# Whole-row accumulations, a fifth product buffer and later gate sums in a Mamba, attention and expert kernel on one core

## The chip, the core and the metric

The kernel runs on one core of one Trainium2 chip, as one launch. The metric is the device time in microseconds; lower is better. The time before is 3446.69 us, the median of three runs (3444.32 to 3450.47). The core has the engines PE (TensorE matmul, with PEld for its weight loads), DVE (VectorE), ACT (ScalarE), POOL (GpSimd) and SP (SyncE, which here only issues DMAs).

## The reference, cut to what matters

The input is 8 images of 256 channels by 32 x 32, that is 8 sequences of 1024 tokens. Layer 0 is a Mamba block and an MLP; layer 1 is attention and a mixture of experts. All is float32. The part that the change touches is the scan of the Mamba block:

```python
xz = x @ W_in
xm, z = jnp.split(xz, 2, axis=-1)            # d_inner = 512 each
xm = silu(causal_conv4(xm) + conv_b)
dt, Bm, Cm = jnp.split(xm @ W_x, [16, 32], axis=-1)
dt = softplus(dt @ W_dt + b_dt)
A = -jnp.exp(A_log)                           # (512, 16)
def step(h, inputs):
    dt_t, B_t, C_t, x_t = inputs
    dA = jnp.exp(dt_t[..., None] * A)
    h = dA * h + (dt_t * x_t)[..., None] * B_t[:, None, :]
    y = jnp.einsum('bds,bs->bd', h, C_t)
    return (h, y)
_, ys = jax.lax.scan(step, h0, seq)
y = (ys + xm * D_param) * silu(z)
x = y @ W_out + residual
# then: x = gelu(layernorm(x) @ W1 + b1) @ W2 + b2 + x
# layer 1: t = t + attention(ln(t)); t = t + experts(ln(t)), two of eight experts per sequence
```

## The kernel before, in words

A sequence is cut into two chunks of 512 tokens, so there are 16 chunks, `i = 0..15`; an even one is a first chunk (`c = 0`) and an odd one the second chunk of its sequence. Channels lie on the 128 partitions, 512 inner channels being four groups, handled as two halves `h` of two groups. A tile of a half is 128 partitions by 2 x 512 values, 0.5 MB.

The scan is written as a stream of 512 steps. A chunk has 32: 16 states `s`, and for each both halves. Step `g` consists of these VectorE operations, written out by hand in the main loop at the end of the function:

- `inputs(g + 1)`: the B product, `hb <- xm,bc`, into a buffer `hb` of the pool `h4`
- `scan(g, q)`: the recurrence by `tensor_tensor_scan`, in place in `hb`, with the decays `da_all` that ScalarE makes in `decay`. A first chunk starts at state zero, and both groups of a half go through one scan of 1024 columns (the first decay of the second group is zero). A second chunk needs two scans of 512, each from the `state` that the first chunk left. In a first chunk GpSimd copies the last column to `state`.
- `sums(g)`: the C product in place in `hb`, and then a DMA issued by GpSimd that adds `hb` to `dx`, the accumulator `me["acc", h]` of this chunk and half. When it has landed the buffer goes back to `h4`.

Sixteen states are thus summed by 512 accumulating DMAs of half a megabyte. `h4` has four buffers. In a first chunk the C product and the DMA leave out the last column (511 of 512), because `state` takes it before the product; the epilogue adds it separately: `yl` is `state` times the last row of C, summed over the states into the accumulator's last column.

Everything else is put around the stream. Each other piece of work is a Python generator: `prologue(i)` (projection, convolution, time step `dt`; ends with `xm <- xm,dt`), `gate_part(i)` (the gate), `epilogue(i)` (output projection and MLP), `attention`, `experts`, `setup` (weights and edge bias, including `column_bias`), and `park`. `park` runs through chunks 2 to 15 once, early and at lowest urgency: it makes their x projection and gate, and stores them in DRAM (`xin_d`, `sz_d`), from which the prologue and `gate_part` load them. The time step needs logarithms, and adds their parts by DMAs issued by GpSimd (`dt <- e`, `dt <- u`).

The order in which generators are advanced is set at build time by a small planner: `Model` and `Queue` keep a clock per engine from fixed prices, `advance()` takes all generators that are due, in order of urgency, until the clock of the work has reached VectorE's (`vec.at`); `keep_warm()` puts filler matmuls (`warm`) where TensorE would stand idle. Each engine then runs its instructions in the order emitted. Four tables of one number per chunk steer it: `FRONT[i]` is the step of chunk `i` in which `prologue(i + 1)` starts, `GATE[i]` that in which `gate_part(i)` starts, `CONV[i]` puts the convolution on TensorE instead of VectorE, and `SOFT[i]` makes a prologue use one more accumulating DMA per half in place of one VectorE operation. `Slots` hands out buffers: `now()` takes the one that is free first, even if that lies ahead of the planner's clock.

At the start the first chunk's input and the weights are loaded. `fold(w, n, gain, ...)` multiplies columns of the input weights `w_in` by the layer norm's gain and makes their column sums with the shift on TensorE (`b_in <- vecs,w_in`, matmuls of one column): once for the x half and, first in `setup`, once for the gate half. `setup` is advanced once while the loads are issued, which emits the gate's column sums.

Of the kernel before, what the change touches and what calls it, by code (L numbers as in the profile page):

```python
# [9 lines left out]
F32 = mybir.dt.float32  # L10
# [3 lines left out]
ALU = mybir.AluOpType  # L14
AX = mybir.AxisListType
PSUM = bass.MemoryType.PSUM

P = 128
B, C, L = 8, 256, 1024
KC = C // P  # L20
CH = 512
NCH = L // CH
DI, NS, RK, KW = 512, 16, 16, 4
ND = DI // P
# [3 lines left out]
NHALF = ND // 2  # L28
# [26 lines left out]
def hybrid_kernel(ctx: ExitStack, tc: tile.TileContext, a: dict, out: bass.AP):  # L55
# [80 lines left out]
    def load(name, shape, src):  # L136
        t = const.tile(shape, F32, name=name, tag=name)
        loads.append((t, src))
        return t
# [7 lines left out]

    work = ctx.enter_context(ExitStack())
    work.enter_context(tc.manual_schedule(engines=set(ENGINES)))
    w_in = load("w_in", [P, KC, 2 * DI], a["W_in"].rearrange("(k p) n -> p k n", p=P))  # L150

    w_x = const.tile([P, ND, 4 * RK], F32, name="w_x")
    w_dt = const.tile([3 * RK, NHALF, P], F32, name="w_dt")
# [114 lines left out]
    T4, H4, PT, AHEAD, LAG, TICK = 25, 4, 4, 2, 8.0, 0.15  # L268


    FRONT = (5, 5, 4, 4, 1, 13, 15, 1, 13, 1, 11, 1, 4, 5, 9)
    GATE = (27, 5, 30, 30, 30, 17, 28, 11, 28, 27, 9, 22, 29, 28, 10, 26)
    CONV = (0, 0, 0, 0, 1, 0, 0, 0, 0, 0, 0, 1, 0, 1, 0, 0)
    SOFT = (1, 1, 1, 1, 0, 0, 0, 0, 0, 0, 0, 0, 0, 0, 0, 0)

# [251 lines left out]
    def fold(w, n, gain, shift, bias, name, first=0):  # L529


        ps = sbank(f"{name}_{first}")
        cols = slice(first * P, (first + n) * P)
        for o in range(n):
            for k in range(KC):
                pe.matmul(
                    ps[:, o : o + 1], w[:, k, cols][:, o * P : (o + 1) * P], V(shift, k),
                    start=(k == 0), stop=(k == KC - 1),
                )
        yield  # L540
        if name == "b1":
            vec.tensor_tensor(bias, ps[:, :n], V("b1"), ALU.add)
        else:
            vec.tensor_copy(bias[:, first : first + n], ps[:, :n])
        for k in range(KC):
            vec.tensor_scalar(w[:, k, cols], w[:, k, cols], V(gain, k), None, ALU.mult)
# [137 lines left out]
    def prologue(i: int):  # L684
# [23 lines left out]
        def skip_path():  # L708

            for h in range(NHALF):  # L710
                dx = me["acc", h] = yield from mem.take(f"dx_{i}_{h}")
                for r in range(2):
                    act.activation(
                        dx[:, r, :], xm[h][:, r, :], AF.Identity, scale=V("D", 2 * h + r)
                    )

        if i == 0:
            yield from skip_path()
# [160 lines left out]
    def place(g):  # L879
        i, k = divmod(g, NSTEP)  # L880
        s, h = divmod(k, NHALF)
        return i, s, h
# [18 lines left out]
    def inputs(g):  # L901

        i, s, h = place(g)
        hb = hbs[g] = h4.now(f"hb_{g}")
        bc, landed = bcs[g // NHALF]
        vec.at = max(vec.at, landed)
        xd = chunk[i]["xd"][h]
        vec.tensor_tensor(hb, xd, bc[:, 0, :].unsqueeze(1).to_broadcast([P, 2, CH]), ALU.mult)
        if s == NS - 1:
            t4.put(xd)  # L910
# [24 lines left out]
    def sums(g):  # L935

        i, s, h = place(g)
        me = chunk[i]
        bc, _ = bcs[g // NHALF] if h < NHALF - 1 else bcs.pop(g // NHALF)
        hb = hbs.pop(g)  # L940
        n = CH if i % NCH == NCH - 1 else CH - 1
        y = hb[:, :, :n]
        vec.tensor_tensor(y, y, bc[:, 1, :n].unsqueeze(1).to_broadcast([P, 2, n]), ALU.mult)
        model.t = vec.at
        me["landed", h] = pool.dma_start(out=me["acc", h][:, :, :n], in_=y, accum_op=ALU.add)
        h4.put(hb, at=me["landed", h])

    parked, parked_x = {}, set()
# [1 line left out]
    def park():  # L950

        for i in range(PARK, B * NCH):
            b, c = divmod(i, NCH)
            sz_d = dram.tile([NHALF, P, 2, CH], F32, name=f"sz_d_{i}", tag=f"sz_d_{i}")
            mem = Owner(t4, 3)
            xn = yield from mem.take(f"xe_{i}")
            yield sp.dma_start(xn, x_v[b, :, :, c * CH : (c + 1) * CH])
            xn = yield from layernorm(mem, banks, xn, xn, f"a{i}", kept=i)
            yield
            xi = yield from gates(i, mem, xn, 0)  # L960
            yield
            for h in range(NHALF):
                mem.put(
                    xi[h], at=sp.dma_start(xin_d[b][h, :, :, c * CH : (c + 1) * CH], xi[h])
                )
            parked_x.add(i)
            sz = yield from gates(i, mem, xn)
            mem.put(xn)
            for t in sz:
                act.activation(t, t, AF.Silu)  # L970
            lnexp()
            yield
            for h in range(NHALF):
                mem.put(sz[h], at=sp.dma_start(sz_d[h], sz[h]))
            mem.end()
            parked[i] = sz_d

    def gate_part(i):

# [22 lines left out]
    def gates(i, mem, xn, first=ND):  # L1002

        while first and not gates_ready:
            yield POLL
        sz, ps = [], None
        for d in range(ND + 1):
            if d:
                h, q = divmod(d - 1, 2)
                act.activation(  # L1010
                    sz[h][:, q, :], ps, AF.Identity, bias=b_in[:, first + d - 1 : first + d]
                )
                banks.put(ps)
            if d < ND:
                if d % 2 == 0:
                    sz.append((yield from mem.take(f"z{first}_{i}_{d // 2}")))
                ps = yield from banks.take(f"z{first}_{i}_{d}")
                for k in range(KC):
                    pe.matmul(
                        ps, w_in[:, k, (first + d) * P : (first + d + 1) * P], xn[:, k, :],  # L1020
                        start=(k == 0), stop=(k == KC - 1),
                    )
                yield
        return sz

    def epilogue(i: int):
# [9 lines left out]
        y = me["sz"]  # L1036
        if c < NCH - 1:
            for h in range(NHALF):
                yl = work_pool.tile([P, NS + 1, 2], F32, name=f"yl_{i}_{h}", tag="yl")
                vec.tensor_tensor(  # L1040
                    yl[:, 1:], state[:, :, 2 * h : 2 * h + 2],
                    me["c_last"].unsqueeze(2).to_broadcast([P, NS, 2]), ALU.mult,
                )
                vec.tensor_reduce(
                    yl[:, 0], yl[:, 1:].rearrange("p s d -> p d s"), AX.X, ALU.add
                )
                y_end = me["acc", h][:, :, CH - 1]
                vec.tensor_tensor(y_end, y_end, yl[:, 0], ALU.add)
        for h in range(NHALF):
            yield me["landed", h]  # L1050
            vec.tensor_tensor(y[h], me["acc", h], y[h], ALU.mult)
            t4.put(me["acc", h])
        yield
# [1006 lines left out]
    with tc.tile_pool(name="work", bufs=1) as work_pool:  # L2060
# [86 lines left out]
        def setup():  # L2147
            mem = Owner(t4, 9)
            tiles = []
            for n in range(9):  # L2150
                tiles.append((yield from mem.take(f"setup_{n}")))
            held = []
            for n in range(2):
                held.append((yield from pairs.take(f"setup_p{n}")))
            pl = Scratch([t4.of[id(t)][1] for t in tiles])
            yield from fold(w_in, ND, "ln1_g", "ln1_b", b_in, "b_in", ND)
            gates_ready.append(True)
            yield
            yield from column_bias(pl)
            yield  # L2160
            eye = pl.tmp("eye", [P, P], F32)
            make_identity(nc, eye)
            blk = pl.tmp("eye_b", [P, HD], F32)
            yield
            for r in range(4):
                rows = slice(HD * r, HD * r + HD)
                vec.tensor_copy(blk[rows, :], eye[rows, rows])
            vec.tensor_tensor(
                taps, blk.unsqueeze(1).to_broadcast([P, ND * KW, HD]),
                V("conv_w").unsqueeze(2).to_broadcast([P, ND * KW, HD]), ALU.mult,  # L2170
            )
            vec.tensor_tensor(pick3, eye[:, 0:4], eye[:, 4:8], ALU.add)
            vec.tensor_tensor(pick3, pick3, eye[:, 8:12], ALU.add)
            set_up.append(True)
            yield
            yield from fold(w1, HID // P, "ln2_g", "ln2_b", b1, "b1")
            yield
            yield from bounds(pl)
            yield
            yield from values_bias(pl)  # L2180
            expert_constants(pl)
            mem.put(*tiles)
            mem.end()
            pairs.put(*held)
# [9 lines left out]
        next(first)  # L2194
        for n, (t, src) in enumerate(loads):
            sp.dma_start(t, src)
            if n == 2:
                next(second)

        folding = fold(w_in, ND, "ln1_g", "ln1_b", b_in, "b_in")  # L2200
        for n in range(8):
# [329 lines left out]
```

## Time and profile before

| What | Value |
|---|---|
| median of three runs | 3446.69 us |
| the profiled execution itself | 3453.02 us |
| its span, first to last instruction | 3451.2 us |
| mean granted TensorE clock | 0.954 |
| PE busy | 3158.2 us, 92% |
| DVE busy | 2994.9 us, 87% |
| ACT busy | 2461.8 us, 71% |
| POOL busy | 1136.1 us, 33% |
| DMA | 667.94 MB, queue 0 (issued by POOL) 57.9% and queue 1 (by SP) 25.1% of 16 engines |

The page of a profile cuts the span into 40 slices and gives each engine's busy share of a slice in tenths. Its groups of instructions name engine, operation and tiles (output, arrow, inputs), with busy time and mean duration, and then the idle time of the engine just before them and what ended it. Nearly all instructions go through one recording helper, so all have its line and the tile names tell them apart. For a DMA the last number is the median time from issue to landing. Durations come from one execution, which took 6.3 us longer than the median. Idle time of an engine that doesn't set the pace costs nothing.

### The profile page before, as it was taken

Reading aid. Unit: us, or ns where it says so; the run is one execution under the profiler, and the core shown is the slowest. Engines: PE = TensorE matmul, PEld = TensorE weight load, DVE = VectorE, ACT = ScalarE, POOL = GpSimd, SP = SyncE. Lnnn points to the kernel's source line nnn. Section 1 sums busy time; section 2 is a strip of 40 time slices with the busy share of each in tenths; the row PEclk is TensorE's granted clock in tenths of the full one; section 3 lists DMA queues with packets and bytes.
Section 4 is the critical chain, followed back from the end, with each engine's and each line's share of the span. In section 5 each row is a group of like instructions: output and inputs, shape, how many; then the busy total and the mean of one; then the engine's idle time right before and its main releaser. Section 6 shows DMA issues by size and latency. Waiting matters only on the chain. (4 is left out here: it accounts for less than half of the span.)

```text
span 3451.2 us, 44547 instructions
## 1 busy us (share of the span) xinstructions
PE 3158.2 (92%) x16321; PEld 1383.4 (40%) x16321; DVE 2994.9 (87%) x3140; ACT 2461.8 (71%) x3594; POOL 1136.1 (33%) x1072
## 2 busy tenths in 40 slices
PE   7888878899999998999999899999899999999997
PEld 5544343433344433433443334333333343335343
DVE  5989999899999979999999999999899899962561
ACT  4667757678868887787768767877768877764643
POOL 0243135312452235332542244225422553311010
PEclk9878998999999999999989999999999999999999
DMA  3888898989899989888998999899978998863140
GB/s 117 224 198 192 201 235 208 223 214 224 200 247 220 239 188 213 198 200 200 220 238 195 210 238 223 191 201 233 205 184 198 232 216 199 209 150 97 32 99 24
DMA packets 248629, 667.94 MB, mean 194 GB/s; under 512 B 31184, under 2 KB 108112, under 8 KB 248400
## 3 DMA queue, kind: packets, MB, share of 16 engines
q0 software_dynamic: 138880, 373.62, 57.9%
q1 hardware_dynamic: 109520, 291.38, 25.1%
q8 instruction: 130, 2.13, 0.2%
q14 instruction: 99, 0.81, 0.1%
HBM read 269.20 MB, written 92.93 MB: 105 GB/s over the span
## 5 line engine op out<-in xcount | busy, mean ns | idle before, releaser
L95 POOL DMA_DIRECT2D dx<-hb x512 | 541.9, 1064 | 1559.2 <-DVE hb L98 1094.7
L98 ACT ACTIVATE da_all<-dt,vecs 128x512 f32<-128x512 f32 (+1 forms) x1024 | 697.2, 716 | 341.8 <-DVE hb L98 333.5
L98 DVE TENSOR_TENSOR hb<-xm,bc 128x1024 f32<-128x1024 f32 x512 | 616.5, 1204 | 52.2 <-DMA dx<-hb 34.2
L98 DVE TENSOR_TENSOR_SCAN hb<-da_all,state,hb 128x512 f32<-128x512 f32 x512 | 631.3, 1268 | 6.4 <-ACT da_all L98 6.4
L98 DVE TENSOR_TENSOR hb<-hb,bc 128x1024 f32<-128x1024 f32 (+1 forms) x512 | 622.4, 1216 | 0.0
L98 DVE TENSOR_TENSOR_SCAN hb<-da_all,hb 128x1024 f32<-128x1024 f32 x256 | 585.0, 2285 | 9.7 <-ACT da_all L98 9.5
L98 ACT ACTIVATE pt<-sc 128x1024 f32<-128x1024 f32 x512 | 494.0, 1017 | 72.0 <-PE sc L98 61.3
L98 PE MATMUL warm<-mean_c,zero_c 128*128 128x256 f32 x1168 | 375.2, 444 | 61.6 <-ACT dt L98 12.0
L98 POOL COPY state<-hb 128x2 f32<-128x2 f32 x256 | 353.7, 1383 | 205.5 <-DVE hb L98 192.2
L98 PE MATMUL sc<-qk,qk 32*128 32x512 f32 x2048 | 327.7, 645 | 11.8 <-ACT pt L98 10.7
L98 PEld LDWEIGHTS warm<-mean_c,zero_c 128*128 128x128 f32 x1168 | 221.1, 210 | 220.5 <-PE warm L98 81.0
L98 PE MATMUL num<-pt,v 128*32 128x512 f32 x2048 | 276.8, 610 | 7.4 <-DVE ot L98 5.9
L98 PE MATMUL facc<-fh,w 128*128 128x512 f32 x512 | 245.5, 630 | 17.4 <-ACT he L98 4.5
L98 PE MATMUL fh<-x_f,w 128*128 128x512 f32 x480 | 232.8, 615 | 10.5 <-DVE x_f L98 5.0
L98 PE MATMUL den<-pt,ecb 128*32 128x512 f32 x1792 | 236.8, 599 | 0.0
L98 PE MATMUL re<-he,g 128*128 128x512 f32 x472 | 216.4, 602 | 10.0 <-ACT x L98 4.2
L98 PE MATMUL he<-xe,g 128*128 128x512 f32 x448 | 219.4, 615 | 4.6 <-DMA xe<-xf_d 4.2
L98 PE MATMUL z<-sq_a,w_in 128*128 128x512 f32 x448 | 216.1, 615 | 3.0 <-ACT z L98 1.2
L98 ACT ACT_TABLE_LOAD x159 | 204.0, 1283 | 3.4 <-PEq L2518 0.7
L98 PEld LDWEIGHTS sc<-qk,qk 32*128 32x128 f32 x2048 | 97.0, 185 | 181.8 <-issue 74.6
L98 PEld LDWEIGHTS facc<-fh,w 128*128 128x128 f32 x512 | 100.0, 202 | 148.6 <-issue 121.3
L98 PEld LDWEIGHTS fh<-x_f,w 128*128 128x128 f32 x480 | 86.0, 191 | 146.6 <-issue 106.3
(410 smaller groups left out, 4141.1 us busy)
## 6 DMA issues: line engine op xcount, KB each, us to landing
bc<-bc_d SPq DMA_DIRECT2D x256, 512.0 KB
dx<-hb POOLq DMA_DIRECT2D x256, 512.0 KB, 7.1
dx<-hb POOLq DMA_DIRECT2D x256, 511.0 KB, 8.0
dt<-e POOLq DMA_DIRECT2D x36, 512.0 KB, 7.7
dt<-u POOLq DMA_DIRECT2D x30, 512.0 KB, 10.8
xin_d<-z SPq DMA_DIRECT2D x28, 512.0 KB
sz_d<-z SPq DMA_DIRECT2D x28, 512.0 KB
sz<-sz_d SPq DMA_DIRECT2D x28, 512.0 KB
```

The costliest lines, as they stand in the source:

```text
L95: f(*args, **kw)
L98: return f(*args, **kw)
```

## The change

- `sums` adds the whole `hb` to the whole accumulator in first chunks as well. The last column then receives values of no meaning. The prologue saves the last column of the freshly made `dx` in a small tile `dx_end` (one ACT copy per half), the epilogue reduces `yl` into the same tile, and after the accumulations have landed it overwrites the accumulator's last column with the sum of both.
- The input weights become two tiles, `w_in` (x half) and `w_z` (gate half), each with its load. When `park` and the first two gates are done, `w_z` is no longer read and joins `h4` as a fifth buffer. `inputs` moves the planner's VectorE clock on to the time when a buffer is free.
- The gate's column sums are no longer emitted while the loads are issued. They come when `setup` is first advanced.
- `FRONT`, `GATE`, `CONV` and `SOFT` have other values.

```diff
-    w_in = load("w_in", [P, KC, 2 * DI], a["W_in"].rearrange("(k p) n -> p k n", p=P))
+    w_in = load("w_in", [P, KC, DI], a["W_in"].rearrange("(k p) n -> p k n", p=P)[:, :, :DI])
+    w_z = load("w_z", [P, KC, DI], a["W_in"].rearrange("(k p) n -> p k n", p=P)[:, :, DI:])
...
-    FRONT = (5, 5, 4, 4, 1, 13, 15, 1, 13, 1, 11, 1, 4, 5, 9)
-    GATE = (27, 5, 30, 30, 30, 17, 28, 11, 28, 27, 9, 22, 29, 28, 10, 26)
-    CONV = (0, 0, 0, 0, 1, 0, 0, 0, 0, 0, 0, 1, 0, 1, 0, 0)
-    SOFT = (1, 1, 1, 1, 0, 0, 0, 0, 0, 0, 0, 0, 0, 0, 0, 0)
+    FRONT = (7, 13, 4, 4, 1, 14, 10, 1, 13, 1, 10, 6, 1, 5, 10)
+    GATE = (20, 4, 30, 30, 22, 7, 30, 18, 28, 25, 5, 28, 30, 30, 12, 26)
+    CONV = (0, 0, 0, 1, 1, 0, 0, 0, 0, 0, 0, 0, 0, 1, 0, 0)
+    SOFT = (1, 0, 0, 1, 0, 0, 0, 0, 1, 0, 1, 0, 0, 0, 0, 0)
...
+                if c < NCH - 1:
+                    if h == 0:
+                        me["dx_end"] = work_pool.tile(
+                            [P, 2, NHALF, 2], F32, name=f"dxe_{i}", tag="dxe", bufs=2
+                        )
+                    act.copy(me["dx_end"][:, 0, h, :], dx[:, :, CH - 1])
...
     def inputs(g):
         i, s, h = place(g)
+        vec.at = max(vec.at, min(h4.free)[0])
         hb = hbs[g] = h4.now(f"hb_{g}")
...
-        me["landed", h] = pool.dma_start(out=me["acc", h][:, :, :n], in_=y, accum_op=ALU.add)
+        me["landed", h] = pool.dma_start(out=me["acc", h], in_=hb, accum_op=ALU.add)
...
+        while not {("g", i) for i in range(PARK)} <= done:
+            yield POLL
+        make = h4.make
+        h4.make = lambda nm, k: w_z if k == H4 else make(nm, k)
+        h4.free.append((model.t, H4))
...
                 vec.tensor_reduce(
-                    yl[:, 0], yl[:, 1:].rearrange("p s d -> p d s"), AX.X, ALU.add
-                )
-                y_end = me["acc", h][:, :, CH - 1]
-                vec.tensor_tensor(y_end, y_end, yl[:, 0], ALU.add)
+                    me["dx_end"][:, 1, h], yl.rearrange("p s d -> p d s"), AX.X, ALU.add
+                )
         for h in range(NHALF):
             yield me["landed", h]
+            if c < NCH - 1:
+                vec.tensor_tensor(
+                    me["acc", h][:, :, CH - 1], me["dx_end"][:, 0, h], me["dx_end"][:, 1, h],
+                    ALU.add,
+                )
...
-            yield from fold(w_in, ND, "ln1_g", "ln1_b", b_in, "b_in", ND)
+            yield from fold(w_z, ND, "ln1_g", "ln1_b", b_in, "b_in", ND)
...
         for n, (t, src) in enumerate(loads):
             sp.dma_start(t, src)
-            if n == 2:
-                next(second)
```

More of the change, by code (lines that the diff above doesn't have):

```diff
@@ L532, in fold @@
         ps = sbank(f"{name}_{first}")
-        cols = slice(first * P, (first + n) * P)
+        cols = slice(0, n * P)
         for o in range(n):
@@ L1019, in gates @@
                     pe.matmul(
-                        ps, w_in[:, k, (first + d) * P : (first + d + 1) * P], xn[:, k, :],
+                        ps, (w_z if first else w_in)[:, k, d * P : (d + 1) * P], xn[:, k, :],
                         start=(k == 0), stop=(k == KC - 1),
@@ L1038, in epilogue @@
             for h in range(NHALF):
-                yl = work_pool.tile([P, NS + 1, 2], F32, name=f"yl_{i}_{h}", tag="yl")
+                yl = work_pool.tile([P, NS, 2], F32, name=f"yl_{i}_{h}", tag="yl")
                 vec.tensor_tensor(
-                    yl[:, 1:], state[:, :, 2 * h : 2 * h + 2],
+                    yl, state[:, :, 2 * h : 2 * h + 2],
                     me["c_last"].unsqueeze(2).to_broadcast([P, NS, 2]), ALU.mult,
```

## The prediction

> **What bounds the kernel now.** I read the busy slices first, then busy time by stretches of the span, then what VectorE waited for in each stretch. The times give where the scans begin (74.8 us) and where VectorE's last scan ends (about 3066). Columns of the first block: stretch and its length, busy time of PE, PEld, DVE, ACT, POOL with instruction counts, TensorE clock, DMA share, GB/s.
>
> ```profile
> 0.00:75.00 75.00, 54.67 (x273) 35.88 (x275) 38.72 (x70) 30.74 (x49) 1.71 (x16) 0.89 0.41 128
> 75.00:325.00 250.00, 211.57 (x1192) 122.72 (x1189) 219.24 (x280) 163.37 (x342) 90.51 (x94) 0.86 0.80 196
> 325.00:1263.00 938.00, 849.82 (x4195) 374.07 (x4194) 878.17 (x820) 704.32 (x1009) 300.51 (x279) 0.95 0.91 218
> 1263.00:3068.00 1805.00, 1685.03 (x8937) 687.73 (x8936) 1714.79 (x1687) 1372.91 (x1947) 703.12 (x643) 0.96 0.93 211
> 3068.00:3451.00 383.00, 357.09 (x1738) 163.04 (x1737) 143.97 (x286) 190.45 (x249) 40.22 (x41) 0.99 0.27 64
> ```
>
> Three stages follow. A start of 75 us; a stream of 512 scan steps, 75 to 3068, in which VectorE is busy 219 + 878 + 1715 = 2812 of 2993 us, so it sets the pace and leaves 181 us idle; and a tail of 383 us in which TensorE is busy 357. TensorE's share in the stream is 92%, part of it `warm` filler. So a gain must come out of the 181 us, or out of the start.
>
> VectorE's waits in the stream from 1250 on (waited for: total us, times, longest), then the group that waits, from the page:
>
> ```profile
> DVE hb L98 <- DMA dx<-hb: 26.3, 15, 4.8
> DVE xm L98 <- DMA dt<-u: 12.2, 2, 10.3
> DVE hb L98 <- issue: 10.2, 4, 4.0
> DVE sz L98 <- DMA dx<-hb: 4.2, 2, 2.7
> ...
> L98 DVE TENSOR_TENSOR hb<-xm,bc 128x1024 f32<-128x1024 f32 x512 | 616.5, 1204 | 52.2 <-DMA dx<-hb 34.2 <-issue 18.1
> dx<-hb POOLq DMA_DIRECT2D x256, 512.0 KB, 7.1
> dx<-hb POOLq DMA_DIRECT2D x256, 511.0 KB, 8.0
> ```
>
> The reader is to see one product, `hb<-xm,bc`, waiting 52 us in all for a free `hb` buffer: the accumulating DMA that last read it hasn't landed. Between a product's hand-over and the reuse of its buffer four steps later VectorE has three scans, two B products and two C products: 3 x 2.29 + 2 x 1.20 + 2 x 1.22 = 11.7 us. Issue (0.9 to 1.2 us) and landing (median 7 to 8, longest 17.3) mostly fit in that, so the waits are short and scattered.
>
> DMA by chunk; queue 0 in a first chunk (1630 to 1817), then in the second chunk after it (1817 to 1989), with packets, MB, share:
>
> ```profile
> q0 software_dynamic: 11298, 25.48, 74.4%
> ...
> q0 software_dynamic: 6259, 22.16, 65.3%
> ```
>
> With queue 1 (25.8%) the first chunk's engines are at 100%.
>
> The start and one chunk border (start us, us, engine, what, idle before it):
>
> ```profile
> 8.22 3.55 PE L98 MATMUL b_in<-vecs,w_in 128*128 128x1 f32 x16 [8.22 <-DMA w_in<-in_W_in]
> 11.70 1.08 PE L98 MATMUL mu_a<-xn,mean_c 128*32 128x128 f32 x16
> ...
> 1232.36 1.23 DVE L98 TENSOR_TENSOR xm<-xm,dt 128x1024 f32<-128x1024 f32 x1 [8.18 <-ACT dx L98]
> ```
>
> The first line are the gate's column sums; the mean of the first chunk stands behind them in TensorE's order. The last is part of the largest stall, 1212 to 1237: the time step of chunk 6 isn't ready.
>
> **What the Trainium skill says.** "DMA: Bandwidth & Descriptors", section "SWDGE vs HWDGE vs iDMA": an accumulating DMA can be issued from GpSimd only, and packets of up to 4096 B are preferred. The trace agrees on the first: all 512 stand in POOL's queue. A whole row pair is 4096 B, a cut one two pieces of 2044 B; the packet counts above fit that. The same page, "Anatomy of one DMA", gives 2.0 us + bytes/436e3, an estimate of 3.2 us for 512 KB. The trace has 7.1: engines that are 90% busy queue. The section "Why small descriptors are slow" says that SBUF-to-SBUF transfers don't suffer from small pieces; the trace differs (8.0 against 7.1 us, and the next part), and I take the trace.
>
> **The change part by part**, against the profiled execution (3453.0 us, span 3451.2; 6.3 above the median of 3446.7).
>
> *Whole rows.* 256 accumulations turn from 2 x 2044 B to 4096 B per partition. Price: queue 0 took 0.744 x 187 x 16 = 2226 engine-us in the first chunk, 0.653 x 172 x 16 = 1797 in the next. At the latter's 81 per MB the former's 25.48 MB would cost 2066: 160 less. Three later pairs give 145, 129 and 238. Of a chunk's 184 x 16 = 2944 that is 4 to 8 points of share. Issue on POOL falls from 1.20 to 0.86 us (its medians in a first and a second chunk). Neither is on VectorE's path; they make landings earlier by about 0.9 us. Before 1250 this alone acts on 15.7 us of `hb` waits (52.3 - 36.5): I take -5; bounds 0 and -10. Waits of `sz` and `dt` on DMAs (4.2 and 15.7 in the stream): -5, bounds 0 and -10; the 10.3 us one at 2698 comes behind a row of gathers on POOL, which stays.
>
> *Fifth slot.* By the recorded order of the changed program 63 of the 512 products use the second half of the input weights, the first in step 196 (about 1285 us). A fifth slot adds one step, 2.29 + 1.20 + 1.22 = 4.7 us, to the 11.7. The longest wait after 1250 is 4.8 us; only where two follow within two steps does something remain (I keep 3). So 36.5 - 3: -34. Lower bound of the gain: no DMA lands earlier, and waits pass on to the serial accumulation per `dx` half (POOL waited 275 us for it in 69 cases), half, -17; upper -36.
>
> *Gate sums later.* TensorE's mean no longer stands behind 3.55 us of sums and the wait to 8.2. The input's DMA issues at 1.2 us, ahead of the weights; at the 330 GB/s and more that this stretch moves, its 0.5 MB have landed by about 5.5 to 6. The next join is `var_a` at 18.4, behind the other column sums, which stay and need only half the weight bytes. I take -5, bounds -2 and -7. The moved sums land among filler after the first convolution, which covers them; the weight load becomes two DMAs on SP (one more issue, 0.5 us, with the small loads behind it; none is needed before 40 us). Two foldings of 0.48 us stay where they were on VectorE.
>
> *The last column.* 16 ACT copies of about 0.19 us: 3 us on an engine busy 76%, hidden; cover gone, +3. VectorE's three small operations per half (0.19 + 0.19 + 0.16) stay in number; the last now follows the landing, which the product after it waits for anyway: 0.
>
> *Planner and tables.* The slot wait is now in the planner's clock, and the tables FRONT, GATE, CONV and SOFT are new. Both tables keep three chunks each, so operations keep their counts: recorded order, equal but for 19 more filler matmuls. What moves is place. I weighed useful TensorE work by the trace's durations (0.87 us for 128x512, about 0.3 for a score, 0.27 for a num or den): 97 us before and 107 after in steps 176 to 191, where TensorE is 199 of 204 us busy (1059 to 1263). That window, the one with the large stall, I lengthen by 10 us; bounds 0 and +25. The prologue there starts one step later (FRONT 13 to 14), its x projection reaches TensorE in step 184 instead of 181, but the products that need it stay in step 189. Elsewhere the sums of 16 steps differ by up to 11 us, in both directions. After the last step the work is the same within 2 us, so the tail keeps its 383.
>
> *Denser stream.* TensorE has 30 us less for the same work: more of VectorE's small waits on PE and ACT (about 60 us in the stream): +5, bounds 0 and +20.
>
> Sum: -5 - 5 - 34 - 5 + 10 + 5 = -34, so 3419 on the profiled execution's scale and 3412.7 on the median's: **3412 us**.
>
> **The rivals.** *Waits move.* TensorE is at 92% in the stream, and a VectorE that no longer waits for slots runs into late layer norms and time steps. For it: TensorE at 199 of 204 us in one window. Against it: in the stream VectorE waits on nothing for long but buffers and that border. Then only the start and a third of the slot gain remain: -5 - 11 + 5, 3436.
>
> *The stream is bound by DMA more than it shows.* With 4 to 8 points taken off a saturated queue, `bc` loads, parked rows and `dt` sums come earlier as well, and half of the remaining idle time in first chunks goes: another -25, about 3387. For it: shares of 100% in first chunks. Against it: few VectorE waits name a DMA.
>
> *The new tables put work where TensorE is full* (slower). Place: steps 176 to 191 and the chunk borders. The time step that is late there holds all scans back, and nothing else fills VectorE. Price: the prologue's three-step delay, 15 us, plus the 10 us of work, at each of two or three borders, 50 to 75, against a gain of 44 to 49: it decides once two such borders appear, and gives about 3446 + 15 to 30, 3470. For it: the stall of 25 us at chunk 6 and of 10 at chunk 14 stand on margins of one step or none. Against it: by the recorded order the last `dt` sum stands as many steps ahead of its product after as before at nearly every border (none at chunk 6, one at chunk 14, two to six elsewhere).
>
> *The fifth slot doesn't take.* It waits for the parked part to be done; the order shows it used from step 196, so this is excluded, but for its benefit.
>
> **How the numbers follow.** Gain as summed, 0.60; DMA relief beyond it, 0.12; waits that move, 0.13; tables that cost, 0.15. Under 0.2% (6.9 us) is about what a measurement of this kernel can't tell from no change. Faster holds the first two and about half of the third: 0.78; same the rest of it with a thin edge of the others, 0.08; slower 0.14. The bounds of the first case, all at one end together, are -63 and +29; mostly it lies in 3385 to 3440. The range reaches down to 3378, into the DMA case, and up to 3447, over the moved waits; outside lie the slower case and some 0.04 below.
>
> **What would show it.** In the profile after: `hb<-xm,bc` idle below 20 us instead of 52.2, under 6 after step 196; both forms of `dx<-hb` one row at about 7 us; under-2-KB packets down by some 65,000; first scan at 68 to 70; last scan near 3030; tail 375 to 390. It is wrong if VectorE's stream idle stays above 165 us with the `hb` waits gone, or if chunk 6's stall passes 40 us.

## The result and the profile after

The changed kernel takes 3406.32 us (median of four runs, 3395.24 to 3419.88) against 3447.68 beside it (3444.32 to 3450.47): ratio 0.9882, interval 0.9839 to 0.9926. A second measurement on another chip, listed below, gave 0.9872 (0.9857 to 0.9888). So the gain is 41 to 44 us by these ratios, where 34 was forecast. The profiled execution took 3395.24 us, 11 below its median; its span is 3393.4, so 57.8 us lie between the two profiles.

The first block is the profile after by stretches, in the columns of the prediction's first block: the start, chunk 0 with the first steps of chunk 1, on to chunk 6, the rest of the stream, and the tail.

```profile
0.00:67.00 67.00, 51.15 (x266) 33.19 (x270) 38.77 (x70) 31.28 (x51) 1.71 (x16) 0.92 0.48 143
67.00:319.00 252.00, 213.68 (x1214) 123.15 (x1215) 236.33 (x299) 173.76 (x352) 82.28 (x94) 0.91 0.76 199
319.00:1230.00 911.00, 841.27 (x4340) 370.34 (x4339) 852.88 (x787) 682.95 (x992) 289.78 (x272) 0.96 0.89 218
1230.00:3011.00 1781.00, 1677.21 (x8792) 698.86 (x8790) 1720.26 (x1702) 1394.04 (x1976) 690.26 (x651) 0.97 0.92 216
3011.00:3393.00 382.00, 358.00 (x1762) 161.48 (x1754) 145.50 (x286) 185.79 (x241) 40.52 (x41) 0.99 0.27 65
```

VectorE's work in the stream hasn't changed (236 + 853 + 1720 = 2809 us; 2812 before); what shrank is the time around it.

Next, from the page: the two groups of the B product (the second in the fifth buffer, `w_z`), the accumulating DMAs and the packet count.

```profile
L98 DVE TENSOR_TENSOR hb<-xm,bc 128x1024 f32<-128x1024 f32 x449 | 540.0, 1203 | 22.5 <-issue 19.8
L98 DVE TENSOR_TENSOR w_z<-xm,bc 128x1024 f32<-128x1024 f32 x63 | 75.7, 1202 | 0.1
dx<-hb POOLq DMA_DIRECT2D x449, 512.0 KB, 7.8
dx<-w_z POOLq DMA_DIRECT2D x63, 512.0 KB, 6.7
DMA packets 216134, 668.21 MB, mean 197 GB/s; under 512 B 31200, under 2 KB 42592, under 8 KB 215904
```

Then VectorE's longest sums of waits in the stream.

```profile
DVE hb L98 <- issue: 19.8, 5, 5.2
DVE xm L98 <- ACT dx L98: 14.0, 1, 14.0
DVE hb L98 <- ACT da_all L98: 12.4, 11, 3.0
DVE e L98 <- ACT u L98: 10.9, 12, 3.6
```

The product waits 22.6 us instead of 52.2, and the 63 uses of the fifth buffer have 0.1 of it. Of the 22.5 in `hb`, the profile puts 2.5 to a landing and 19.8 to `issue`, which means that it names nothing that ended the wait. These five waits are for buffers too, as far as the trace shows: many landings aren't recorded in it, but three of the five, 13.9 us, end within 0.1 us after the landing of an accumulation. Two of the five, 9.7 us, follow a train of gathers (indirect DMAs that fetch the experts' weights) on POOL; two others, 9.0 us, come at 524 and 616 us, before the first gather at 1033. Packets under 2 KB fell by 65,520 from 108,112. What is left at the top are these five waits and waits for ScalarE.

Queue 0 of the DMA engines in a first chunk (1583 to 1773) and the second chunk after it (1773 to 1949), by queue:

```profile
q0 software_dynamic: 7558, 26.37, 71.5%
...
q0 software_dynamic: 6577, 23.67, 68.4%
```

The timeline of the start and of the border to chunk 6:

```profile
5.25 1.08 PE L98 MATMUL mu_a<-xn,mean_c 128*32 128x128 f32 x16 [5.25 <-DMA xn<-in_x]
...
1208.97 1.23 DVE L98 TENSOR_TENSOR xm<-xm,dt 128x1024 f32<-128x1024 f32 x1 [13.99 <-ACT dx L98]
```

A first chunk now costs 0.715 x 190 x 16 / 26.37 = 82 engine-us per MB on queue 0, like a second chunk (81), where it was 87. The mean starts when the input has landed, at 5.25 instead of 11.70. The longest wait at the border is 14.0 us instead of 8.2; VectorE idles 18.6 us from 1180 to 1215, where it idled 20.9 from 1205 to 1240.

For every kernel below, the trace gives one table. Stream: from the first scan to the end of the last; idle: that length less VectorE's busy time in it (2809 to 2814 us in all of them); product: idle time of the B product (`hb<-xm,bc` and `w_z<-xm,bc`); other: idle less product; tail: what follows. All in us, each from one profiled execution; the ratio comes from the medians.

| kernel | first scan | stream | idle | product | other | tail | ratio to before (interval) |
|---|---|---|---|---|---|---|---|
| before | 74.8 | 2988.7 | 177.5 | 52.2 | 125.3 | 387.8 | 1 |
| after | 66.8 | 2946.4 | 134.5 | 22.6 | 111.9 | 380.2 | 0.9882 (0.9839, 0.9926) |
| after_again | 68.0 | 2947.4 | 135.6 | 26.2 | 109.4 | 381.9 | 0.9872 (0.9857, 0.9888) |
| a6_order_only | 72.0 | 2989.6 | 176.0 | 86.5 | 89.5 | 382.3 | 1.0009 (0.9998, 1.0021) |
| a1_four_real | 67.2 | 2975.8 | 162.7 | 65.3 | 97.5 | 380.0 | 0.9925 (0.9910, 0.9941) |
| a2_cut_rows | 67.6 | 2956.4 | 144.5 | 30.7 | 113.8 | 380.2 | 0.9883 (0.9861, 0.9905) |
| a4_sums_early | 73.4 | 2952.7 | 140.1 | 27.4 | 112.7 | 381.0 | 0.9855 (0.9836, 0.9874) |
| b2_five_real | 74.9 | 2957.8 | 147.9 | 15.9 | 132.0 | 390.4 | 0.9925 (0.9907, 0.9943) |
| b4_late_sums | 70.2 | 2984.1 | 174.4 | 53.1 | 121.3 | 393.0 | 0.9976 (0.9964, 0.9988) |
| b5_new_tables | 74.4 | 3022.7 | 208.4 | 44.1 | 164.4 | 391.8 | 1.0179 (1.0166, 1.0192) |
| a5_no_planner_wait | 67.7 | 3016.8 | 203.8 | 13.8 | 190.0 | 387.9 | 1.0059 (1.0044, 1.0074) |
| a3_old_tables | 71.6 | 3070.2 | 256.9 | 18.8 | 238.1 | 387.1 | 1.0210 (1.0197, 1.0223) |
| c1_spread | 71.9 | 2942.7 | 133.8 | 11.1 | 122.7 | 402.7 | 0.9887 (0.9865, 0.9908) |
| c4_front13 | 71.2 | 3004.3 | 192.0 | 14.6 | 177.3 | 387.1 | 0.9999 (0.9984, 1.0013) |

### The profile page after: what moved, and what is told of

It reads as the page before. It is cut to its first block, busy times and chain, and to the rows that moved or that the text cites. A ratio compares the mean times of both kernels' runs of the same rounds, so it can differ in the third digit from the quotient of the medians.

```text
span 3393.4 us, 44585 instructions
## 1 busy us (share of the span) xinstructions
PE 3141.3 (93%) x16359; PEld 1387.0 (41%) x16359; DVE 2993.7 (88%) x3140; ACT 2467.8 (73%) x3610; POOL 1104.5 (33%) x1072
## 5 line engine op out<-in xcount | busy, mean ns | idle before, releaser
L95 POOL DMA_DIRECT2D dx<-hb x449 | 397.3, 890 | 1363.5 <-DVE hb L98 960.8
L98 DVE TENSOR_TENSOR hb<-xm,bc 128x1024 f32<-128x1024 f32 x449 | 540.0, 1203 | 22.5 <-issue 19.8
L98 DVE TENSOR_TENSOR_SCAN hb<-da_all,state,hb 128x512 f32<-128x512 f32 x448 | 552.7, 1268 | 4.2 <-ACT da_all L98 4.1
L98 DVE TENSOR_TENSOR hb<-hb,bc 128x1022 f32<-128x1022 f32 (+1 forms) x449 | 546.7, 1218 | 0.0
L98 DVE TENSOR_TENSOR_SCAN hb<-da_all,hb 128x1024 f32<-128x1024 f32 x225 | 514.2, 2285 | 8.3 <-ACT da_all L98 8.3
L98 PE MATMUL warm<-mean_c,zero_c 128*128 128x256 f32 x1182 | 366.0, 433 | 48.9 <-ACT z L98 11.5
L98 POOL COPY state<-hb 128x2 f32<-128x2 f32 x225 | 330.6, 1471 | 206.4 <-DVE hb L98 201.2
L98 PE MATMUL sc<-qk,qk 32*128 32x512 f32 x2048 | 337.7, 647 | 18.2 <-ACT pt L98 17.1
L98 PE MATMUL num<-pt,v 128*32 128x512 f32 x2048 | 279.6, 616 | 13.2 <-DVE ot L98 13.2
L98 PE MATMUL facc<-fh,w 128*128 128x512 f32 x512 | 232.8, 601 | 5.9 <-ACT fo L98 2.4
L98 PEld LDWEIGHTS re<-he,g 128*128 128x128 f32 x472 | 89.9, 196 | 133.2 <-issue 103.8
L98 PEld LDWEIGHTS fh<-x_f,w 128*128 128x128 f32 x480 | 86.5, 190 | 133.9 <-issue 100.3
## 6 DMA issues: line engine op xcount, KB each, us to landing
dt<-u POOLq DMA_DIRECT2D x30, 512.0 KB, 11.4
```

Source lines behind the costliest of these rows:

```text
L95: f(*args, **kw)
L98: return f(*args, **kw)
```

## The experiments

Kernels named a and c are edits of the kernel after, those named b of the kernel before. Theory: the fifth buffer and the whole rows take the product's waits away, and the order of the other work costs or saves little. Rival: the gain comes from the order.

**a1_four_real.** The planner counts five buffers, so every engine's order is after's; in truth four are used in turn.

```diff
-        h4.make = lambda nm, k: w_z if k == H4 else make(nm, k)
+        turns = iter(range(10**6))
+        h4.make = lambda nm, k: make(nm, next(turns) % H4)
```

> The changed kernel with every engine's order of instructions unchanged; only the memory behind the five slots is four buffers taken in turn, so the fifth slot exists for the planner alone. Theory 1 (the missing buffer cost VectorE time): the product's wait for a free buffer, 22.5 us in all in the changed kernel's profile, returns to 40 to 60 us, most of it after 1250 us, and the time is 20 to 35 us above the changed kernel's 3406, about 3430. Rival (the new order of work brings the gain and the buffer only shifts waits to TensorE and ScalarE): within 8 us of 3406.

Measured: 3425.21 us, ratio 0.9925. The B product on its page:

```profile
L98 DVE TENSOR_TENSOR hb<-xm,bc 128x1024 f32<-128x1024 f32 x512 | 617.1, 1205 | 65.3 <-DMA dx<-hb 51.3
```

Up to chunk 6 its chunks begin within 2.2 us of after's; from there on, where the fifth buffer is missing, it falls behind by 28 us. The medians make it 0.43 to 0.53% against the two ratios of after, 15 to 18 us; the expectation of theory 1 had 20 to 35, and 40 to 60 us of waits where 65.3 came. It is also more than the 8 us of the rival.

**a2_cut_rows.** After's order, but first chunks accumulate 511 columns again.

```diff
-        me["landed", h] = pool.dma_start(out=me["acc", h], in_=hb, accum_op=ALU.add)
+        pool.at = max(pool.at, model.t) + 1.0
+        nc.gpsimd.dma_start(out=me["acc", h][:, :, :n], in_=y, accum_op=ALU.add)
+        me["landed", h] = model.move(pool.at, P * 2 * CH * 4, True)
```

> The changed kernel with its order unchanged; in first chunks the accumulating DMA again leaves out the last column (511 of 512, two pieces of 2044 B). Theory 1 (shorter DMAs relieve queue 0): packets under 2 KB rise by 65,000, queue 0's share by about 3 points, issue on POOL from 0.86 to 1.2 us, and the time is 8 to 20 us above 3406, seen in the even chunks. Rival (landings are early enough once a fifth buffer is there): under 5 us.

Measured: 3409.73 us, 0.9883, 108,128 packets under 2 KB again. Its page has both kinds of row side by side:

```profile
dx<-hb POOLq DMA_DIRECT2D x225, 511.0 KB, 8.0
dx<-hb POOLq DMA_DIRECT2D x224, 512.0 KB, 7.7
```

With five buffers the whole rows bring 0 to 4 us by the medians, within the intervals of nothing: the rival's figure. The traces show more, 9 to 10 us less idle time with whole rows (134.5 and 135.6 against 144.5), and the intervals don't exclude that either.

**a4_sums_early.** After, with the gate's column sums emitted during the loads again.

```diff
+            if n == 2:
+                next(second)
```

> The changed kernel with the gate's column sums again emitted while the loads are issued; the other engines keep their order. Theory: the first scan moves from 66.9 back to about 73 us and the whole time by the same 5 to 7 us, since VectorE sets the pace from there on. Rival (the setup's indirect loads, not VectorE, end the first chunk, so a later start is absorbed in chunk 0): first scan later by 6 us, chunk 1's first scan by under 2.

Measured: 3403.62 us, 0.9855; the first scan came at 73.4 instead of some 67, yet the median is no higher than after's. The rival's account doesn't explain that: in the trace chunk 1's first scan is 6.2 us later too (311.3 against 305.1), where the rival had under 2, and the delay is still 6 us at chunk 6. Why the medians don't show it stays open.

**b2_five_real.** Before, with split input weights and five buffers in turn once the parked part is done; tables, planner's clock and cut rows stay as before.

```diff
+        def five(nm, k):
+            k = next(turns) % (H4 + 1)
+            return w_z if k == H4 else make(nm, k)
+        h4.make = five
```

> The kernel before with its order of instructions, its tables and its cut rows; only the input weights are two tiles, and after the parked part the products go through five buffers in turn instead of four, without the planner knowing. Theory 1: the product's waits after 1250 us fall from 36.5 to under 8 us and the time by 20 to 32 us, to 3415 to 3428. Rival (waits move: TensorE and ScalarE are just as late): the product's waits go, others grow by as much, and the time stays within 8 us of 3447.

Measured: 3426.08 us, 0.9925, 26 us. Its product waits:

```profile
L98 DVE TENSOR_TENSOR hb<-xm,bc 128x1024 f32<-128x1024 f32 x448 | 539.1, 1203 | 13.8 <-DMA dx<-hb 7.5 <-issue 6.2
L98 DVE TENSOR_TENSOR w_z<-xm,bc 128x1024 f32<-128x1024 f32 x64 | 77.0, 1204 | 2.1 <-DMA dx<-w_z 1.4 <-issue 0.4 <-POOL state L98 0.3
```

So on before's order 36.3 us of product waits go, and the other waits grow by 7. The fifth buffer is worth 26 us there without any part of the rest.

**after_again.** The kernel after once more, beside the next three.

> The changed kernel once more, beside the variants of this set on one chip. All theories: 0.986 to 0.990 of the kernel before.

Measured: 3401.60 us, 0.9872.

**b5_new_tables, a5_no_planner_wait, a3_old_tables.** Before with the four new tables alone; after without the line `vec.at = max(vec.at, min(h4.free)[0])`; and after with before's four tables.

> The kernel before with the four new tables and nothing else. Theory A (they only fit the changed planner's clock): no gain, or slower by up to 20 us. Theory B (they are better starts in themselves): 15 to 25 us faster than before, in chunks 0 to 4.

> The changed kernel without the line that moves the planner's VectorE clock on to a free buffer; the real buffers, the tables and the rows stay as changed. With four real buffers and the new order the time was still 0.75% below the kernel before, so some 26 us come from the order of work. Theory A (the planner's clock brings them: work is then issued for a VectorE that waits): 15 to 25 us above the changed kernel. Theory B (the tables bring them): within 8 us of it.

> The changed kernel with the four tables FRONT, GATE, CONV and SOFT of the kernel before; planner clock, five buffers and whole rows stay. Theory A: within 8 us of the changed kernel. Theory B: 15 to 25 us above it, with the first five chunks (1016 us to chunk 5's first scan) longer by 15 us or more.

Measured: 3507.69 us (1.0179), 3469.18 us (1.0059) and 3519.34 us (1.0210). The waits of the last, which are to be held against after's above:

```profile
DVE xm L98 <- DMA dt<-u: 44.2, 7, 11.7
DVE hb L98 <- ACT da_all L98: 32.6, 17, 5.0
DVE e L98 <- ACT u L98: 21.6, 8, 7.0
DVE xm L98 <- ACT dx L98: 20.5, 2, 12.8
```

Buffers are not the matter here: the product waits only 18.8 us. The time step comes late: seven waits for `dt<-u` where after has three, and they are longer. The new tables and the planner's clock belong together; either without its partner costs 68 to 118 us against after. The direction is theory A's for b5 and a5 and theory B's for a3, but every loss is several times the size expected, and the premise of the second text, that some 26 us come from the order, falls with the next run. That a3 loses early, as theory B said, holds: it comes to chunk 5 42 us later than after_again.

The prediction's slower rival named the border to chunk 6, and there it shows in part where the new tables stand without the planner's line: chunk 5 takes 231 us in b5 and in a5, against 197.5 before and 205.5 after. That is 34 us at one such border, where the rival counted on 25 at two or three; so it is chance that a5, at 3469, is near its 3470.

**a6_order_only.** The edits of a1, a2 and a4 at once: after's order, with before's four buffers, cut rows and early sums.

> The changed kernel's order of instructions, with its three local parts taken out at once: four product buffers in turn, first-chunk accumulations that leave out the last column, gate sums back in the first loads. What is left of the change is the order alone (new tables, waits in the planner's clock). If the parts add up (fifth buffer 24, whole rows 0 to 7, late sums 0 to 6 us), it comes to 3430 to 3438, some 10 to 18 us faster than before. If the order alone carries the gain that the fifth buffer doesn't, it is below 3430. If whole rows matter once only four buffers are there (rows that land later, with no slack), it is above 3440, no gain, and waits of hb for DMAs exceed 65 us.

Measured: 3457.32 us, 1.0009: no gain. The adding up of single parts (3430 to 3438) fails, and the time is that of the last of the three expectations, above 3440. Its sign, over 65 us of waits for DMAs, is met only if the waits without a named cause count with the 61.5 that the profile puts to landings. Its product:

```profile
L98 DVE TENSOR_TENSOR hb<-xm,bc 128x1024 f32<-128x1024 f32 x512 | 618.5, 1208 | 86.5 <-DMA dx<-hb 61.5
```

In these traces the order alone takes 36 us of other waits away (125.3 to 89.5) and puts 34 onto the product (52.2 to 86.5). It is a trade, and only buffers that come free sooner cash it. Against a1, whole rows and late sums together now bring 0.84%, 29 us (20 to 38 by the interval ends), though with five buffers neither showed anything. So whole rows and the fifth buffer are substitutes in part: each shortens the same waits. In the new order the product waits 86.5 us with neither, 65.3 with whole rows and late sums, 30.7 with the fifth buffer and late sums, and 22.6 with all three. (The profiled execution of a6 was 11.5 us below its median, so that the trace shows less than the medians.)

**b4_late_sums.** Before with the split weights and the late sums alone.

```diff
-            yield from fold(w_in, ND, "ln1_g", "ln1_b", b_in, "b_in", ND)
+            yield from fold(w_z, ND, "ln1_g", "ln1_b", b_in, "b_in", ND)
...
-            if n == 2:
-                next(second)
```

> The kernel before with one part alone: the input weights in two loads and the gate column sums moved behind the first convolution. The rest of the order, tables and buffers are before's. The prediction's step: first scan some 5 us earlier and all of it kept, ratio 0.9985 (3443). The run of the changed kernel with early sums says: first scan 7 us earlier, and the gain lost by the first chunk borders, because the prologue of the next chunk and not the start sets the pace there: within 2 us of before, ratio 0.9995 to 1.001.

Measured: 3445.91 us, 0.9976, 8 us (4 to 12); first scan 4.6 us earlier in the traces. The first of the two expectations holds on before's order, as nearly as the interval tells. Taking 8 from the 29 leaves about 20 for the whole rows with four buffers; that subtraction wasn't run by itself.

**c1_spread.** Two of after's five `issue` waits stand behind trains of gathers on POOL. The timeline of the kernel after (start, duration) for POOL, and then for VectorE's product that waits for it:

```profile
2439.58 2.01 POOL L95 DMA_INDIRECT g<-eW_d,rows  x1 [0.30 <-issue]
2441.89 2.97 POOL L95 DMA_INDIRECT g<-eW_d,rows  x1 [0.30 <-DVE w_z L98]
2444.86 1.02 POOL L95 DMA_DIRECT2D fo<-x1m_d  x1
2445.46 1.34 POOL L95 DMA_DIRECT2D dx<-hb  x1
...
2453.76 1.22 DVE L98 TENSOR_TENSOR hb<-xm,bc 128x1024 f32<-128x1024 f32 x1 [5.22 <-issue]
```

These are the last two of six gathers; the accumulation behind them is issued late and takes 8.2 us to land, and the product starts 0.1 us after that, having waited 5.2 us. The edit lets other work in between, after each gather of `g1` and `g2`:

```diff
+                yield model.t + 4.5
```

> The changed kernel with the twelve weight gathers of an expert put 4.5 us apart on POOL instead of in trains of six, so that an accumulation never stands behind more than one. If these trains are what the remaining issue waits of hb (20 us in five places) come from, those fall below 8 us and the run gains 5 to 12: 3392 to 3400 where the changed kernel has 3405. The rival: the planner, which orders everything after these gathers anew, puts time steps or joins later, as in the runs with unmatched tables; then it loses, by 10 to 60 us, while the issue waits fall all the same.

Measured: 3418.17 us beside a before of 3454.32, 0.9887: no gain over after. `Issue` waits fell from 19.8 to 11.1, not below 8: the two behind gathers are gone, and 10.5 us are left in the two at the places of 524 and 616 us, which no gather precedes. VectorE's other waits grew by as much (111.9 to 122.7), so that its idle time in the stream is the same (133.8 against 134.5). The tail, which starts at 3014.5 here and at 3013 in after, grew:

```profile
3014.50:3417.00 402.50, 376.11 (x1782) 168.89 (x1778) 146.10 (x288) 202.22 (x263) 43.45 (x44) 0.98 0.28 65
```

and the same stretch of after:

```profile
3013.00:3393.00 380.00, 356.00 (x1742) 161.06 (x1738) 143.50 (x285) 184.35 (x240) 38.70 (x40) 0.99 0.26 64
```

20 us more of TensorE work were left for after the last scan. So the trains of gathers are shown as the cause of those two waits, not of all five, and taking them away brought no time: what they gave was spent on other waits.

**c4_front13.** After with one table entry put back.

```diff
-    FRONT = (7, 13, 4, 4, 1, 14, 10, 1, 13, 1, 10, 6, 1, 5, 10)
+    FRONT = (7, 13, 4, 4, 1, 13, 10, 1, 13, 1, 10, 6, 1, 5, 10)
```

> The changed kernel with one table entry put back: the prologue of chunk 6 starts at step 13 of chunk 5 instead of step 14. If the prediction was right that the later start holds up this border (a wait of 14 us for dx is left there), chunk 5 gets shorter by 5 to 14 us, and the rest stays: 3393 to 3400. If the table is a fitted set, in which every entry only holds for the order that the others make, chunk 5 may gain and a later border loses more: 3410 to 3460, with late time steps (xm for dt, hb for da_all) in chunks 6 to 14.

Measured: 3455.04 us, 0.9999: all of the gain gone, by one entry. The wait at the border to chunk 6 stayed (13.2 us), so the prologue's later start isn't what makes it; chunk 5 got longer (212.0 against 205.5), and so did chunks 11, 13 and 14. Not all of the trace's difference is the entry's: at chunk 5's first scan, up to which both kernels run the same instructions, c4 is already 13.6 us behind (1029.6 against 1016.0), at a lower clock (0.92 against 0.94). Its waits are of a3's kind:

```profile
DVE xm L98 <- ACT dx L98: 20.1, 3, 13.2
DVE e L98 <- ACT u L98: 19.7, 12, 8.0
DVE xm L98 <- DMA dt<-u: 17.7, 4, 7.5
```

No run here beats the kernel after beyond its interval.

## Why the prediction was right, step by step

**What bounds the kernel** held: VectorE's busy time in the stream is the same in fourteen profiles (2809 to 2814 us), and the stream's length goes with its idle time.

**Fifth slot, -34.** Right on the order it was worked out from: in b2 36.3 us of product waits are gone, 34.4 of them after 1250 us, and 26 us in the medians; 7 us turn up elsewhere. Within the whole change the medians give it 15 to 18. That its share there is smaller isn't shown: the intervals overlap (8 to 29 us, against 20 to 32 in b2), and in the traces VectorE's idle time falls by 28 us from a1 to after and by 30 from before to b2. The product waits 22.6 us in all, where below 20 was said, and 11.4 after step 196, not under 6: 10.8 of it in three `issue` waits, two of which stand behind gathers.

**Whole rows, -5 and -5.** Packets, share (4 points of a first chunk: 0.715 stands for 0.758 at 87 per MB) and issue on POOL (0.86 us) came as told; the size was off. About -20 with four buffers, by subtraction, and 0 to -4 with five. The step that failed is the landing, 0.9 us earlier. The 8.0 and 7.1 us of before were from first and from second chunks, and the difference is that of the chunks: in after, where all rows are whole, a first chunk's accumulations land in 7.9 us and a second chunk's in 7.2 (medians of those recorded), and a2's cut rows in 8.0. The Trainium skill, "DMA: Bandwidth & Descriptors", section "Why small descriptors are slow", says that SBUF-to-SBUF transfers don't suffer the penalty of small pieces. The landings agree with it, and so do the medians as long as buffers are plenty (0 to 4 us of 3410 in a2); the engines' time doesn't (87 against 82 engine-us per MB), and with four buffers that seems to show in time too.

**Gate sums, -5.** First scan 8.0 us earlier in the two profiles, a bit past the bound of 7; but part of that isn't the step's. c4 has the same instructions at the start as after, and its first scan comes at 71.2 instead of 66.8: from 20 to 40 us it was granted 0.74 of the clock, after 1.00. Where the clock of that stretch was alike (0.91 to 0.92) the step is 4.6 us (before against b4) and 5.4 (a4 against after_again), as forecast. In the medians it is -8 alone on before's order (4 to 12), and nothing to be seen in the changed kernel (a4).

**Planner and tables, +10.** The number was near (a6: +3, from -1 to +7), and chunk 5 did get longer as said: 197.5 before, 205.5 after, 207.7 in a6 (the prologue's later start isn't the reason, by c4). The mechanism failed. The step asked where the order puts work that is late, and not what the order does to the buffers: it freed 36 us of other waits and made 34 of product waits. So the sum's base of 52.2 us of product waits was too small. The 10.3 us wait at 2698, said to stay, went with the order (longest `dt<-u` 3.5 in a6 and in after), as did 5.5 us of the tail (387.8 to 382.3), said to keep its length. A slip without effect: `SOFT` marks four chunks in both kernels and `CONV` three, not three each.

**Denser stream, +5.** Mis-sized: from a6 to after the other waits grow from 89.5 to 111.9, by 22. With that, the account of the stream closes on the traces: 64 us of product waits gone from a6, 22 come back, and the net of 42 is close to the 43 by which the stream is shorter.

**The total** came out with some luck: the two effects of the order that the sum left out, 34 us more of product waits and 36 us less of others, cancel, and the remedies then took more than was counted (64 us) while more came back (22). Of the rivals, "waits move" happened to a third of those 64 us, and relief of the DMA engines beyond the sum's 10 us showed only with four buffers. The new tables did not cost together with their planner line (a6); without it they did (a5).

## What to carry to other kernels

When an order is laid out anew together with a change of buffers, take the waits for buffers from the new order with the old buffers (a6), not from the old kernel: an order can trade one kind of wait for the other at no change in time. Two remedies for one wait don't add up; test each with and without the other. Tables fitted to a planner belong to that planner's clock; one entry or one line of it alone may cost more than the whole change brings.

## What was not expected of the hardware

- Time goes with the granted TensorE clock. The four runs of after: 3395.24 us at 0.963, 3398.32 at 0.962, 3414.32 at 0.957, 3419.88 at 0.957. Up to chunk 5's first scan, after and c4 run the same instructions, in 1016.0 us at 0.94 and in 1029.6 us at 0.92. In these traces the clock is either full or half (from 20 to 40 us of c4, 0.50 for 10 us), and the mean counts the halved stretches. Forty runs of before on one chip have 0.950 to 0.958 and on average some 1.1 us less per 0.001, with wide scatter. The median clock of a6 is 0.9535, that of a1 0.9595; at that rate some 7 us of their 29 would go with the clock, an estimate. Which of clock and time is the cause, and what grants the clock, wasn't tried and stays open.
- An accumulation of 512 KB landed hardly sooner for having half the packets (in first chunks 7.9 us whole in after, 8.0 cut in before and in a2) while the engines were some 90% busy.
- An indirect gather held POOL 1.8 to 3.0 us in the train shown, an accumulation in the median 0.9; the six in a row took 15 us (2429.8 to 2444.9), and the accumulation behind them was issued only then.
